# Row LSTM with group norm on one core: part of the second half's first row moved ahead of the last image's statistics, and late work in another order

## The chip, the cores and the metric

One core of a Trainium2 chip runs the whole program. The metric is the device time of one execution in microseconds; lower is better. Four executions of the kernel before give a median of 2064.85 us (2064.63 to 2064.95).

## The reference, cut to what matters

The input x has 8 images of 96 channels, 128 rows and 128 columns, all float32. It is group-normalised (32 groups of 3 channels), convolved along each row with a masked 3-tap filter, and then a convolutional LSTM runs down the 128 rows, one row after another:

```
its = conv(gn(x), W_is * mask) + b_is          # 1 x 3 along a row, 384 gate channels
def step((h, c), row):                          # 128 steps, each needs the one before
    gates = conv(h, W_ss) + b_ss + row          # 3 taps along the row
    f, i, o = sigmoid(...); g = tanh(...)
    c = f * c + i * g
    h = o * tanh(c)
out = x + h of every row
```

The scale and shift of the group norm need the sums of a whole image. So no row of an image can be normalised before all of that image has been read once.

## The kernel before, in words

The 8 images are split into two halves of four (`s` = 0 and 1). A half step `n` is one row of one half: `n = 2 * row + s`. The two halves take turns, so that the gates of one are evaluated while the products of the other run. The 384 gate channels are three tiles A, B, C of 128 rows, each in a PSUM bank of 512 columns: two transforms of 4 images x 64 column pairs, 256 columns each ("half 0" and "half 1" of the bank).

For every tile of a half step there are seven products, each a matmul over 256 columns (4 images x 64), and each of them two instructions on TensorE (PE). `P`, `Q` and `E` (`p_`, `q_`, `t_`) multiply the own part of the normalised input, kept in `xs`; they use 64 of the 128 rows of the array, and two of them on different rows run side by side. `1`, `2`, `0`, `3` (`m1_`, `m2_`, `m0_`, `m3_`) multiply operands made from the previous row's h and the shared part of the input, kept in `hx`: `vs` (sum, `total`, L496), `vf` (difference, `difference`, L500) and `vd` (`shifted`, L504). All products go through `HalfStep.mm` and stand on L390. Then `cp` copies half 0 with its bias, `lo` (L439) and `hi` (L443) combine the halves, and `0`, `3` are added after `lo` and `hi`. `ta` and `si` are the gate functions on ScalarE (ACT), `gt` the product of gates, `th` and `ou` give the new h.

The order on PE, ACT, VectorE (DVE) and GpSimd (POOL) is the order of the program; nothing reorders it. A list such as `"1A 2A PA"` is run by `do(n, names)`; `+` means the next half step and `*` the one after that. So `P*A`, called with n = 1, is the product P for tile A of half step 3, the second row of the second half.

The program has two parts. First all 8 images are read once for their sums (a loop over 8 images and 24 chunks of 512 columns each; DVE's `bn_stats`, L760, and ACT share the chunks). Beside it `events[at(image, chunk)]` places other work: while images 4 to 7 are read, half steps 0 and 2 are begun with the first half's images. Image 7 is the last one; before it is done, the scale of images 4 to 6 is made (`begin_scale`, `squares`, `next_row`), and three of four images of the second half get their first row (`next_operands`, `own_row(..., 0, BH - 1)`).

TensorE is also given products that nobody reads: `spin(count, rhs)` (L174), 256 columns each, into a bank that half step 1 later overwrites; `keep_warm(count)` puts one narrow product in front that waits for the newest record of the statistics.

When image 7's sums are aggregated (`st`, L674), its scale is made. The chain is short instructions on two engines: `final.deviations()` (PE, `dm<-st`, L251), `variance_and_square` (DVE, L272), `variances` and `means` (PE, `pv`, `dm`, L251), `scale` (eight instructions of DVE, L279 to L286), then the last image's shared input (DVE, L782) and its part of `vs` and `vf`. After that the products of half step 1 start. Meanwhile ACT widens the last image's first row (`xw`, L295) and rows 1 to 3 of all four images (`rows`, L295, tile `piece`), and POOL makes the last image's `xs` and `vd`, normalises the shared part of rows 1 to 3 for four images (`shared_rows(nc.gpsimd, 1, 1, R)`, L297, tile `hx`), and combines rows 1, 2 and 3 to `xs` (`own_row`, L315 and L316).

From half step 3 on, a fixed order (`PERIOD`, `PRODUCTS`) repeats to the end.

Of the kernel before, what the change touches and what calls it, by code (L numbers as in the profile page):

```python
# [21 lines left out]
def kernel(  # L22
# [32 lines left out]
    nc = tc.nc  # L55
    B, C, H, W = x.shape
    P = 128
    NH = 2
    BH = B // NH
    R = 4  # L60
    NB = H // R
    J = W // 2
# [23 lines left out]
    wt = [tap[1], wm[:, 0, :], wm[:, 1, :], tap[2]]  # L86
# [44 lines left out]
    xw = [const.tile([P, R, W + 1], F32, tag=f"xw{i}", name=f"xw{i}") for i in range(2)]  # L131
# [29 lines left out]
    E = mybir.EngineType  # L161
# [7 lines left out]


    def spin(count, rhs):
        unread = half_step(1).ps[0]
        for i in range(count):
            nc.tensor.matmul(  # L174
                unread[:, 0 : rhs.shape[1]],
                wt[0][:, 0:P],
                rhs,
                start=True,
                stop=True,
                skip_group_check=True,  # L180
            )

    def first_rows(s, homes=(0, 1, 2)):

        hi = 1 if s else R
        t = xt[s, 0].rearrange("c b r w -> c b (r w)")[:, :, 0 : hi * W]
        own, shared = (x0[:, 0], x0[C:P, 1]) if s else (xr[s], t[C:P])
        for i in homes:
            if i == 2:
                nc.scalar.activation(shared, t[C2:C], AF.Identity)  # L190
            else:
                nc.scalar.activation(own[i * C2 : (i + 1) * C2], t[0:C2], AF.Identity)
# [33 lines left out]
    class Scale:  # L226


        def __init__(self, s, lo, hi, banks=None):
            n, self.name = hi - lo, f"{s}_{lo}"  # L230
            self.st, self.rstd, self.nmr = (
                st[s][:, lo:hi], rstd[s][:, :, lo:hi], nmr[s][:, :, lo:hi]
            )


            self.first, at = banks is None, 0 if banks is None else 3 * BH
            self.banks = banks or [bank(f"{name}{self.name}") for name in ("dm", "pv")]
            self.dm, self.pv = (
                own[:, at : at + i * n].rearrange("p (i b) -> p i b", i=i)
                for own, i in zip(self.banks, (3, 2))  # L240
            )
            self.pm = self.dm[:, 1:3, :]
            self.q, self.t, self.minus = (
                const.tile([P, *shape], F32, name=f"{name}{self.name}")
                for name, shape in (("q", [n]), ("t", [2, n]), ("minus", [2, n]))
            )
            for i in range(2):
                self.mm(self.pv[:, i, :], i, eps[:, 0:n], start=self.first and i == 0)

        def mm(self, o, i, rhs, start=False, stop=False):  # L250
            nc.tensor.matmul(o, gm[:, i, :], rhs, start=start, stop=stop, skip_group_check=True)  # L251
# [47 lines left out]
    def widen(engine, xw, i, n, s, k, j, lo, step=1):  # L299


        norm(
            engine,
            strided(xw[:, i, :], 0, [(step * (W + 1), n), (J + 1, 2), (1, J)]),
            (x0[:, 0, j] if s == 1 and k == lo == 0 else xr[s][:, j, lo * W : (lo + n) * W])
            .rearrange("p (r j t) -> p r t j", r=n, t=2),
            0,
            1,
            s * BH + j,
        )  # L310

    def combine(xw, n, total, differences):

        e, o = xw[:, 0:n, 0:J], xw[:, 0:n, J + 1 :]
        nc.gpsimd.tensor_add(total, e, o)  # L315
        nc.gpsimd.tensor_sub(  # L316
            differences,
            strided(xw[:, 0, :], 0, [(W + 1, n), (J, 2), (1, J)]),
            strided(xw[:, 0, :], J + 1, [(W + 1, n), (0, 2), (1, J)]),
        )  # L320
# [7 lines left out]
    def own_row(xw, s, r, lo=0, hi=BH):  # L328

        to = xs[s][0]  # L330
        combine(
            xw[:, lo:hi],
            hi - lo,
            to[:, r, 0, lo:hi],
            to[:, r, 1:3, lo:hi].rearrange("p t b j -> p b t j"),
        )

    def normalise_shared(engine, s, k, j, lo, hi):

        norm(  # L340
            engine,
            strided(
                hx[s][k % 2][C:P, lo, 0, j, :],
                0,
                [(2 * BH * JP, hi - lo), (BH * JP + 1, 2), (1, J)],
            ),
            (x0[C:P, 1, j : j + 1] if s == 1 and k == lo == 0 else xt[s, k][C:P, j, lo:hi, :])
            .rearrange("p r (j t) -> p r t j", t=2),
            C,
            0,  # L350
            s * BH + j,
        )

    HB = BH * J
    NT = NB * R
    last = NT * NH - 1
    order = {"A": 0, "B": 1, "C": 2}
# [4 lines left out]
    class HalfStep:  # L362


        def __init__(self, n):
            self.n, (self.row, self.s) = n, divmod(n, NH)
            self.ps, self.m1, self.moving, self.done, self.gates = {}, {}, {}, set(), None
            self.started = set()
            self.hx = hx[self.s][self.row // R % 2][:, self.row % R]
            self.xs = xs[self.s][self.row // R % 2][:, self.row % R]  # L370
            self.c = cs[self.s].rearrange("p t b j -> p (t b j)")
# [14 lines left out]
        def mm(self, a, half, weights, rhs, rows=slice(0, P)):  # L386
            self.take_bank(a)
            new = a not in self.started
            self.started.add(a)
            nc.tensor.matmul(  # L390
                self.ps[a][:, bass.ts(half, HB)],
                weights[rows, bass.ts(a, P)],
                rhs[rows],
                start=new,
                stop=False,
                skip_group_check=True,
            )
# [170 lines left out]
    def finish(n):  # L568
# [22 lines left out]
    PARTS = {  # L591
        "P": "p_", "Q": "q_", "E": "t_", "1": "m1_", "2": "m2_", "0": "m0_", "3": "m3_",
        "cp": "copy", "lo": "even", "hi": "odd", "ta": "tanh", "si": "sigmoid",
        "fg": "forget", "gt": "gated", "ce": "cell", "th": "cell_tanh", "ou": "output",
        "S": "total", "F": "difference", "D": "shifted", "re": "residual",
    }
    steps = {}

    def half_step(n):
        if n not in steps:  # L600
            steps[n] = HalfStep(n)
        return steps[n]

    def do(n, names):

        for name in names.split():
            at = n
            for mark, offset in (("'", -1), ("+", 1), ("*", 2)):
                if mark in name:
                    at, name = n + offset, name.replace(mark, "")  # L610
            tile_ = name[-1] if name[-1] in order else ""
            part = name[: len(name) - len(tile_)]

            if part in ("S", "F", "D"):
                at += NH
            if not 0 <= at <= last:
                continue
            step = half_step(at)
            if name not in step.done:
                step.done.add(name)  # L620
                getattr(step, PARTS[part])(*([order[tile_]] if tile_ else []))
# [15 lines left out]
    def shared_rows(engine, s, lo, hi, images=range(BH)):  # L637
        for j in images:
            normalise_shared(engine, s, 0, j, lo, hi)
# [30 lines left out]
    def at(image, n):  # L670
        return image * NS + n
# [4 lines left out]
    def next_products():  # L676
# [5 lines left out]
            half_step(1).take_bank(a)  # L682
        do(2, "PA PB QA QB PC QC 1A 2A 1B 2B 1C 2C")

    def begin_scale():
        late[0].deviations()
        late[0].variances(late[0].st[:, :, 1])
# [6 lines left out]
    def keep_warm(count):  # L694
        spin(1, bst[:, done - 1, :])
        spin(count, wt[0][:, 0:256])
# [16 lines left out]
        ),  # L713
        at(6, 8): lambda: (do(0, "gt th ou"), operands(2), do(0, "re")),
        at(6, 9): next_products,
        at(6, 17): lambda: keep_warm(6),
        at(6, 22): lambda: (first_rows(1), do(2, "cpA cpB cpC")),
        at(7, 5): begin_scale,
        at(7, 7): squares,
        at(7, 8): lambda: (next_row(), spin(14, wt[0][:, 0:256])),  # L720
        at(7, 12): next_operands,
        at(7, 20): lambda: (own_row(xw[1], 1, 0, 0, BH - 1), keep_warm(2)),
        at(7, 22): lambda: keep_warm(2),
    }
    for b in range(B - 1):
# [43 lines left out]
    rows = ring[2][:, 0 : (R - 1) * BH * (W + 1)].rearrange("p (r q) -> p r q", q=W + 1)  # L769
# [4 lines left out]
    final.variance_and_square()  # L774
    final.variances(final.q)
    final.means()
    spin(4, wt[0][:, 0:256])
    nc.scalar.activation(final.minus, final.pm, AF.Identity, scale=-1.0)
    final.scale()
    nc.gpsimd.tensor_mul(final.nmr, final.minus, final.rstd)  # L780
# [9 lines left out]
    step = half_step(1)  # L790
# [6 lines left out]

    for j in range(BH):
        widen(nc.scalar, rows, j, R - 1, 1, 0, j, 1, step=BH)
    shared_rows(nc.gpsimd, 1, 1, R)  # L800
    for r in range(1, R):
        own_row(rows[:, (r - 1) * BH : r * BH], 1, r)
    load_rows(0, 1)
    for s in range(NH):
# [2 lines left out]

    do(1, "1A 2A 1B 2B 1C 2C PA PB QA QB E+A PC E+C QC P*A E+B cpA cpB cpC loA loB loC")  # L810
    do(1, "EA P*B Q*A EB EC Q*B hiA hiB hiC 0A 3A 0B 3B 0C 3C taA taB siB taC siC")
    finish(0)
    do(1, "gt th 0+A 3+A 0+B 3+B 0+C 3+C ou F S D re")
    finish(1)
# [9 lines left out]
    step, halves = half_step(last), [(0, BH // 2), (BH // 2, BH)]  # L824
# [62 lines left out]
```

## Time and profile before

| | |
|---|---|
| median of four executions | 2064.85 us |
| the profiled execution | 2065.23 us, span 2063.5 us |
| PE busy | 1961.2 us, 95% of the span |
| DVE, POOL, ACT busy | 1678.0, 1450.3, 1364.2 us |
| PE's last unbroken stretch | from 153.59 us on, 1899.64 us |
| mean granted TensorE clock | 0.996 |

The span is the time from the first to the last instruction of the profiled execution; 1.7 us of its time lie outside. Line numbers are those of the kernel before. A matmul of the program is two instructions in the profile.

### The profile page before, as it was taken

To read this page: it belongs to the slowest core of one execution; us is meant where nothing else is said; L and a number is where in the kernel's file an instruction comes from. 1 tells how busy PE (TensorE), PEld (TensorE's weight loads), DVE (VectorE), ACT (ScalarE), POOL (GpSimd) and SP (SyncE) were. 2 spreads that over 40 slices of the span, in tenths; PEclk is the share of its full clock that TensorE was granted. 3 is DMA by queue.
4 is the path that set the end of the run, shared out by engine and by line. 5 is a ranking of instruction groups with operands and counts; after the bars stand their busy time and mean duration, and the time that the engine had idled before them with its cause. 6 is when DMAs were issued, how large, how long until landed. Compare 5 with 4: busy or idle time off the path is not lost.

```text
span 2063.5 us, 31403 instructions
## 1 busy us (share of the span) xinstructions
PE 1961.2 (95%) x10866; PEld 1597.4 (77%) x10866; DVE 1678.0 (81%) x3489; ACT 1364.2 (66%) x2403; POOL 1450.3 (70%) x1652
## 2 busy tenths in 40 slices
PE   0389999999999999999999999999999999999998
PEld 0268888888888888888888888888888888888886
DVE  5768888888888888888888888888888888888887
ACT  4776666666666666666666666666666666666666
POOL 3348777777777777777777777777777777777762
PEclk9989999999999999999999999999999999999999
DMA  9994333444333344433334443333444333344411
GB/s 382 424 308 89 94 87 87 109 113 113 94 76 87 87 109 113 113 93 77 87 88 107 113 113 93 77 88 87 107 113 113 96 74 88 88 107 113 113 31 31
DMA packets 103325, 236.26 MB, mean 114 GB/s; under 512 B 5952, under 2 KB 8896, under 8 KB 97280
## 3 DMA queue, kind: packets, MB, share of 16 engines
q1 hardware_dynamic: 103168, 234.25, 41.2%
q8 instruction: 88, 1.44, 0.3%
q14 instruction: 69, 0.57, 0.1%
HBM read 183.90 MB, written 50.33 MB: 114 GB/s over the span
## 4 chain that ended last, share of the span: by engine, by line
PE 94%; DMA 3%; DVE 1%; POOL 1%; ACT 0%; issue 0%; SPq 0%; DVEq 0%; POOLq 0%
PE ps L390 93%; DMA xs<-in_x_dram 3%; DVE bst L760 1%; PE ps L174 1%; POOL xs L315 0%; POOL xs L316 0%; POOL xw L297 0%; SPq L748 0%; POOL hx L297 0%; PE pv L251 0%; ACT xs L217 0%; ACT xs L216 0%; ACT g L446 0%; PE dm L251 0%; ACT ps L453 0%
## 5 line engine op out<-in xcount | busy, mean ns | idle before, releaser
L390 PE MATMUL ps<-vd,wl 128*128 128x256 f32 x3072 | 814.3, 388 | 0.0
L446 ACT ACTIVATE g<-ps 32x512 f32<-32x512 f32 x768 | 454.3, 592 | 449.7 <-PE ps L390 441.6
L390 PEld LDWEIGHTS ps<-vd,wl 128*128 128x128 f32 x3072 | 562.4, 190 | 151.2 <-issue 85.1
L504 POOL TENSOR_TENSOR vd<-hx 128x512 f32<-128x512 f32 x257 | 266.8, 1038 | 460.4 <-DVE vs L496 459.4
L390 PE MATMUL ps<-xs,wx 64*128 64x256 f32 x3072 | 459.4, 395 | 11.0 <-POOL xs L315 11.0
L390 PE MATMUL ps<-vs,wm 128*128 128x256 f32 x1536 | 458.9, 381 | 4.5 <-POOL vs L496 4.4
L390 PE MATMUL ps<-vf,wm 128*128 128x256 f32 x1536 | 458.6, 380 | 0.0
L453 ACT ACTIVATE ps<-ps 96x512 f32<-96x512 f32 x766 | 417.7, 572 | 16.2
L390 PEld LDWEIGHTS ps<-xs,wx 64*128 64x128 f32 x3072 | 323.7, 187 | 119.7 <-issue 83.6
L458 DVE TENSOR_TENSOR ps<-ps,c 96x512 f32<-96x512 f32 x254 | 176.7, 696 | 257.5 <-ACT ps L453 257.4
L443 DVE TENSOR_TENSOR ps<-m,ps 128x256 f32<-128x256 f32 x768 | 329.2, 429 | 26.9 <-PE ps L390 0.7
L522 POOL TENSOR_TENSOR x<-x,hx 96x512 f32<-96x512 f32 x255 | 331.0, 1298 | 5.7 <-DVE hx L483 5.7
L439 DVE TENSOR_TENSOR ps<-m,ps 128x256 f32<-128x256 f32 x768 | 325.1, 424 | 8.9
L390 PEld LDWEIGHTS ps<-vs,wm 128*128 128x128 f32 x1536 | 292.6, 191 | 46.1 <-POOL vs L496 5.4
L390 PEld LDWEIGHTS ps<-vf,wm 128*128 128x128 f32 x1536 | 292.7, 191 | 40.8 <-DVE vf L500 0.4
L436 ACT ACTIVATE m<-ps,wl 128x256 f32<-128x256 f32 x514 | 243.9, 475 | 74.7 <-PE ps L390 61.3
L316 POOL TENSOR_TENSOR xs<-xw 128x512 f32<-128x512 f32 (+1 forms) x254 | 270.7, 1066 | 0.0
L390 PE MATMUL ps<-xs,wt 64*128 64x256 f32 x1530 | 264.5, 376 | 0.1
L476 ACT ACTIVATE th<-c 96x512 f32<-96x512 f32 (+1 forms) x257 | 161.8, 630 | 105.7 <-DVE c L471 104.3
L297 POOL TENSOR_SCALAR hx<-x,rstd,nmr 32x512 f32<-32x512 f32 (+1 forms) x252 | 204.8, 813 | 25.9
L297 POOL TENSOR_SCALAR xw<-xr,rstd,nmr 128x512 f32<-128x512 f32 x252 | 203.7, 808 | 7.7 <-DVE nmr L289 6.7
L390 PEld LDWEIGHTS ps<-xs,wt 64*128 64x128 f32 x1530 | 195.0, 187 | 18.0 <-issue 0.7
(91 smaller groups left out, 1302.2 us busy)
## 6 DMA issues: line engine op xcount, KB each, us to landing
xr<-in_x_dram SPq DMA_DIRECT2D x124, 512.0 KB, 6.4
x<-in_x_dram SPq DMA_DIRECT2D x63, 768.0 KB, 5.9
out_dram<-x SPq DMA_DIRECT2D x62, 768.0 KB, 4.9
xs<-in_x_dram SPq DMA_DIRECT2D x30, 1024.0 KB, 12.4
piece<-in_x_dram SPq DMA_DIRECT2D x16, 1024.0 KB, 12.3
x<-in_x_dram SPq DMA_DIRECT2D x62, 256.0 KB, 3.1
xs<-in_x_dram SPq DMA_DIRECT2D x4, 512.0 KB, 8.5
out_dram<-x SPq DMA_DIRECT2D x2, 576.0 KB, 3.7
```

Of the source, the lines that this page charges most:

```text
L297: engine.tensor_scalar(dst, src, scale, shift, ALU.mult, ALU.add)
L316: nc.gpsimd.tensor_sub(differences, strided(xw[:, 0, :], 0, [(W + 1, n), (J, 2), (1, J)]), strided(xw[:, 0, :], J + 1, [(W + 1, n), (0, 2) ...
L390: nc.tensor.matmul(self.ps[a][:, bass.ts(half, HB)], weights[rows, bass.ts(a, P)], rhs[rows], start=new, stop=False, skip_group_check=True,)
L436: nc.scalar.activation(self.m1[a], m1, AF.Identity, bias=column)
L439: nc.vector.tensor_add(self.ps[a][:, 0:HB], self.m1[a], self.ps[a][:, HB:])
L443: nc.vector.tensor_sub(hi, self.m1[a], hi)
L446: nc.scalar.activation(self.g[a * 32 : (a + 1) * 32], self.ps[a][C:P], AF.Tanh)
L453: nc.scalar.activation(gate, gate, AF.Sigmoid)
L458: nc.vector.tensor_mul(f, f, self.c)
L476: nc.scalar.activation(self.part(self.th, lo, hi), self.part(self.c, lo, hi), AF.Tanh)
L504: diff = nc.gpsimd.tensor_sub(self.operand("vd", 2)[:, :, lo:hi], strided(h, 1, [(BH * JP - 1, 2), (JP, hi - lo), (1, J)]), strided(h, 0, ...
L522: (nc.gpsimd if 2 * row + s < last else nc.vector).tensor_add(xo, xo, self.h)
```

## The change

Seven edits, all around the end of the statistics:

1. `spin` writes to the bank of tile C of half step 1, no longer of tile A.
2. `keep_warm` in image 6 runs 14 unread products, no longer 6.
3. New: `early(names)` runs products of half step 1 on images 0 to 2 alone (192 columns), and leaves the fourth image (64 columns) for the place where the product stood before. At `at(7, 20)` it runs `1A 2A 1B 2B` in place of `keep_warm(2)`.
4. Behind the last image's `means`, `early("PA PB QA QB")` and two unread products stand in place of four.
5. POOL's order: the shared rows of images 0 and 1, then `own_row` of row 1, then the shared rows of images 2 and 3, then rows 2 and 3.
6. The list of half step 1 is split, so that tiles A and B return to 256 columns behind `QB`.
7. Half step 1 runs `hi`, `0`, `3` and the gate functions in the order B, A, C, no longer A, B, C.

```diff
     def spin(count, rhs):
-        unread = half_step(1).ps[0]
+        unread = half_step(1).ps[2]
...
-            self.started = set()
+            self.started, self.images = set(), {}
...
+            lo, hi = self.images.get(a, (0, BH))
+            cols = slice(lo * J, hi * J)
             nc.tensor.matmul(
-                self.ps[a][:, bass.ts(half, HB)],
+                self.ps[a][:, bass.ts(half, HB)][:, cols],
                 weights[rows, bass.ts(a, P)],
-                rhs[rows],
+                rhs[rows, cols],
...
+    def early(names):
+
+        step = half_step(1)
+        for name in names.split():
+            step.images[order[name[1]]] = (0, BH - 1)
+            getattr(step, PARTS[name[0]])(order[name[1]])
+            step.images[order[name[1]]] = (BH - 1, BH)
...
-        at(6, 17): lambda: keep_warm(6),
+        at(6, 17): lambda: keep_warm(14),
...
-        at(7, 20): lambda: (own_row(xw[1], 1, 0, 0, BH - 1), keep_warm(2)),
+        at(7, 20): lambda: (own_row(xw[1], 1, 0, 0, BH - 1), early("1A 2A 1B 2B")),
...
     final.means()
-    spin(4, wt[0][:, 0:256])
+    early("PA PB QA QB")
+    spin(2, wt[0][:, 0:256])
...
-    shared_rows(nc.gpsimd, 1, 1, R)
-    for r in range(1, R):
+    shared_rows(nc.gpsimd, 1, 1, R, range(0, 2))
+    own_row(rows[:, 0:BH], 1, 1)
+    shared_rows(nc.gpsimd, 1, 1, R, range(2, BH))
+    for r in range(2, R):
         own_row(rows[:, (r - 1) * BH : r * BH], 1, r)
...
-    do(1, "1A 2A 1B 2B 1C 2C PA PB QA QB E+A PC E+C QC P*A E+B cpA cpB cpC loA loB loC")
-    do(1, "EA P*B Q*A EB EC Q*B hiA hiB hiC 0A 3A 0B 3B 0C 3C taA taB siB taC siC")
+    do(1, "1A 2A 1B 2B 1C 2C PA PB QA QB")
+    half_step(1).images.clear()
+    do(1, "E+A PC E+C QC P*A E+B cpA cpB cpC loA loB loC")
+    do(1, "EA P*B Q*A EB EC Q*B hiB hiA hiC 0B 3B 0A 3A 0C 3C taB siB taA taC siC")
```

## The prediction, made before the changed kernel ran

> **What bounds the kernel now.** I read the chain of waits first, in order of time, because it shows where the place of the change lies on the path.
>
> ```profile
> span 2063.5 us, 31403 instructions
> 125.04 11.34 PE ps L174 x40
> ...
> 144.97 8.59 PE ps L390 x46
> 153.56 0.03 issue
> 153.59 1899.64 PE ps L390 x10600
> ```
>
> Columns are start, length, what. From 153.59 us the chain is PE alone. In the single records behind it, neighbouring half steps take 7.74 and 7.31 us in turn to the end, and no two matmuls start more than 0.33 us apart. So this part is set by PE, and the change leaves its instructions and their order as they are: it moves as a block, by as much as its start moves. What counts is when the first product of half step 3 starts, now 153.59. Ahead of it, 11.34 us of the chain are products that nobody reads (L174). So I looked at PE and DVE there, each in order of time (start, length; in brackets the idle time before and what ended it):
>
> ```profile
> 124.90 9.30 PE L174 MATMUL ps<-wl 128*128 128x256 f32 x28
> 134.04 0.28 PE L174 MATMUL ps<-bst,wl 128*128 128x6 f32 x2
> 136.21 0.28 PE L251 MATMUL dm<-st,wl 128*128 128x1 f32 x2
> 137.33 0.58 PE L251 MATMUL dm<-st,wl 128*128 128x1 f32 x4
> 139.90 0.67 PE L390 MATMUL ps<-vs,wm 128*128 128x256 f32 x2 [0.15 <-DVE vf L500]
> 144.97 0.48 PE L390 MATMUL ps<-xs,wx 64*128 64x256 f32 x1 [0.31 <-POOL xs L315]
> ```
>
> and on DVE:
>
> ```profile
> 133.31 0.63 DVE L674 BATCH_NORM_AGGREGATE st<-bst 128x2 f32<-128x105 f32 x1
> 136.53 0.28 DVE L272 TENSOR_SCALAR q<-dm,st 128x1 f32<-128x1 f32 x1 [2.59 <-PE dm L251]
> ```
>
> The last image's statistics are there at 133.94 (133.31 + 0.63), but `dm`, which needs them, starts at 136.21: it stands behind the unread products in PE's queue, and DVE idles 2.59 us. Why the queue is late is seen in the granted clock, cut in slices of 1 us (length; busy time of PE, PEld, DVE, ACT, POOL; clock; DMA):
>
> ```profile
> 117.00:118.00 1.00, 0.70 (x4) 0.27 (x2) 1.00 (x2) 1.00 (x3) 0.00 (x0) 1.00 0.99 410
> 121.00:122.00 1.00, 0.08 (x1) 0.12 (x1) 1.00 (x3) 0.76 (x2) 0.00 (x0) 0.50 1.00 426
> 130.00:131.00 1.00, 1.00 (x3) 0.74 (x3) 1.00 (x3) 0.97 (x3) 1.00 (x4) 0.50 0.14 57
> 131.00:132.00 1.00, 1.00 (x6) 0.89 (x5) 1.00 (x3) 0.91 (x2) 0.89 (x4) 1.00 0.34 77
> ```
>
> PE ends image 6's unread products at 117.70 and idles to 121.92. The clock falls to half at 120.8 and stays there to 131.0, so most of the 28 spin instructions start 0.427 us apart, not 0.216. The second thing on the path is the 144.97 row: `P*A` waits for POOL, whose own order holds it up:
>
> ```profile
> 139.82 3.05 ACT L295 ACTIVATE piece<-xr,nmr,rstd 128x384 f32<-128x384 f32 x4
> ```
>
> and on POOL:
>
> ```profile
> 141.13 3.06 POOL L297 TENSOR_SCALAR hx<-x,rstd,nmr 32x384 f32<-32x384 f32 x4
> 144.27 0.64 POOL L315 TENSOR_TENSOR xs<-piece 128x256 f32<-128x256 f32 x1
> ```
>
> The rows that L315 needs leave ACT at 142.87; POOL makes four `hx` first.
>
> **Edit 2, eight more unread products in image 6.** 16 instructions x 0.216 = 3.45 us: PE is busy to 117.70 + 3.45 = 121.15 instead of 117.70, and idles 0.8 us before `dm` of images 4 to 6 (121.92), which they do not delay. The four changes of the clock here (110.5, 113.9, 120.8, 131.0) are 3.41 us or multiples of it apart. The steps of 3.41 us with PE idle for 3 us or more lowered it; the one from 103.7 with 1.1 us idle did not. So I take the clock as kept. The short matmuls then take 0.112 us each (137.33 row: 0.45 for four starts) and not 0.213 as at 122 to 125. The spin starts at about 123.6 and ends at about 129.7. If the clock does fall at 124.2, one full step raises it (110.5 to 113.9 did), and the spin ends at 131.3. [...]
>
> **Edit 3, `1A 2A 1B 2B` on three images, ahead.** Eight instructions of 192 columns, 0.75 x 0.216 = 0.162 each, 1.3 us. `vs` and `vf` of three images leave POOL at 130.07 and 130.65, so these end at 131.9 (132.6 with a clock that fell). Behind them the remaining `keep_warm` waits for DVE's statistics (131.95) and takes 0.22 + 4 x 0.216 = 1.1 us: PE is free at 133.1 to 133.7. Statistics to `dm` took 0.15 us in the earlier case (121.77 to 121.92). So `dm` starts at 133.94 + 0.15 = **134.08, 2.13 us earlier**. DVE's statistics do not move: they wait at 129.43 for the DMA. The chain from `dm` to `1A` keeps its links and its 3.69 us, so `1A` starts at 137.77. DMAs that this uncovers: the row data for ACT was issued by 130.8 and landed within 5.7 us, the `x` piece for `hx` at 131.5 and 6.0 us later: 136.5 and 137.5, needed at 137.7 and 139.0. The 512 KB of the next rows land at 144.7, needed at 147. SP's queue is in the same order; only its last load starts with ACT's earlier end.
>
> **Edit 4, `PA PB QA QB` ahead and two spins fewer.** Between `means` and `1A`: 0.65 + 0.86 instead of 1.73 us, hidden behind DVE's `scale`; `xs` of three images is there at 133.6. If that cover were gone it would cost nothing more than the spins it replaces.
>
> **What the early products save on PE.** The 64 columns left of `1` and `2` cost between 0.054 (a quarter of 0.216) and 0.112 per instruction; I take 0.112, since the nearest row is the short matmuls with a new weight load each. [...] By my row `1A 2A 1B 2B` fall from 1.73 to 0.90 us. `PA PB QA QB` fall from 0.97 to 0.45 (loads side by side) or 0.90 (one by one). From `1A`: 0.90 + 0.86 (1C, 2C) + 0.45 to 0.90 + 0.86 (E+A, PC, E+C, QC) + 0.2 for changes of shape = 3.3 to 3.7. PE is ready for `P*A` at 141.1 to 141.5.
>
> **Edit 5, POOL's order.** `own_row` of row 1 now waits for two `hx` (ended at 142.61 before) and ACT's rows (142.87), so it can start at 142.93 instead of 144.27, **1.34 us earlier** relative to the chain: 142.93 - 2.13 = 140.80, ends 141.44, `P*A` at 141.50. That is later than PE is ready, or just equal: what the early products save on PE is mostly waited away. The two `hx` put behind L316 are needed by half step 3 at 150, when POOL is long done; POOL stood idle 2.29 us before its next `vd`.
>
> **Edit 7, B first.** `hiB` waits for `EB`, which stands behind `Q*A` and so behind L316: before, `hiB` started 1.80 after `P*A` and took 0.43; so `0B` starts 2.27 after `P*A`, where `0A` started 2.085 after it: 0.19 lost. The gates gain: `taA`, `taB`, `siB`, `taC` with a wait of 0.27 become `taB siB taA taC` without. But before, PE was ready at 153.49, only 0.09 ahead of `vf`; so 0.09 of that gain is seen, and then PE is the bound: **+0.10**. Edits 1 and 6 move no time by themselves.
>
> **Sum.** -2.13 - 1.34 + 0.10 = -3.37 us against the profiled execution: 2065.23 - 3.37 = 2061.86. That execution lies 0.38 above the median, so I predict 2061.48, rounded **2061.5**, -0.16%. A measurement of this kernel can tell about 0.2%, 4.1 us, from no change; the forecast is just inside. Its own range is 2060.9 to 2062.1, from the bounds of the narrow products, the 0.15 us start of `dm`, and `hiB`.
>
> **Rivals.** *The clock is not kept* (0.11). If the clock stays at half from 124.2 to 131.0, as it did although PE had been busy from 124.9, the spin ends at 133.0, the early products at 134.3, `keep_warm` at 135.4: `dm` gains 0.81, not 2.13. Time 2061.5 + 1.32 = 2062.8. For it: one full-looking step before did not raise the clock. Against: the idle time that lowered it is filled. *All ends are favourable* (0.20). The loads run side by side, `P*A` comes with PE's 141.1 rather than POOL's 141.5, `hiB` is not late, and the shorter gate chain is all used: 0.4 + 0.2 + 0.2 more, 2060.7 or a little less, over the bound of 0.2%. Against: L315 needs all four widened images. *The moved work waits elsewhere* (0.06). If a transfer for ACT or POOL lands 2 us later than before, the gain of `dm` goes there: 2063.5. *Slower* (0.06): PE now idles 0.6 us before `1A` and does narrow work before that; if this lowers the clock at 137.8 for as long as it stayed low before, 10.2 us, half of that is lost, 5.1 - 3.4 = +1.7: 2066.6. It decides from 6.8 us of half clock on. Against: spins still stand there. The forecast has 0.57.
>
> **Numbers.** The range 2060.2 to 2063.5 takes in the forecast, the first rival, the transfer that comes late and half of the favourable case; 0.16 is left out. Faster by over 0.2% needs the favourable case: 0.22 with a little for what I do not see. Slower by over 0.2%: 0.04. The rest, 0.74, is within 0.2%.
>
> **What would show it.** Right: clock 1.0 from 114 on; `dm<-st` 128x1 at about 134.1; `1A` (128x64) at 137.8; L315 at 140.8 straight behind ACT; `P*A` at 141.5 behind a short wait for POOL; the unbroken PE stretch from about 150.2 and as long as before, 1899.6. Wrong: a half clock after 124, a wait for a DMA at `piece` or `hx`, or another length of the last stretch.

## The result and the profile after

| | before | after |
|---|---|---|
| median | 2064.50 us (52 runs, 2062.09 to 2069.27) | 2062.19 us (34 runs, 2061.19 to 2066.47) |
| profiled execution | 2065.23 us, span 2063.5 | 2064.12 us, span 2062.3 |

The ratio is 0.9990, with a 95% interval of 0.9985 to 0.9994: 2.3 us less, inside the 0.2% that were named as no clear change, and clear of zero. The predicted 2061.5 us is 0.7 us below the median. The profiled execution of after is one of its slower ones, 1.9 us above its median; in it the clock falls, and that turned out to be the key to the case.

The page and the chain of waits of after, in order of time (start, length, what):

```profile
span 2062.3 us, 31445 instructions
145.97 1906.16 PE ps L393 x10630
```

PE again carries all that follows; L393 is the old L390. From half step 3's first product to the end it takes 1909.59 us (1909.57 before). What changed lies ahead of it. PE in order of time:

```profile
114.84 6.29 PE L174 MATMUL ps<-wl 128*128 128x256 f32 x28
122.59 0.36 PE L251 MATMUL dm<-st,wl 128*128 128x3 f32 x2 [1.47 <-DVE st L677]
124.69 9.27 PE L174 MATMUL ps<-wl 128*128 128x256 f32 x28
133.80 0.49 PE L393 MATMUL ps<-vs,wm 128*128 128x192 f32 x2
136.18 0.28 PE L251 MATMUL dm<-st,wl 128*128 128x1 f32 x2
139.79 0.43 PE L393 MATMUL ps<-vs,wm 128*128 128x64 f32 x2
143.69 0.48 PE L393 MATMUL ps<-xs,wx 64*128 64x256 f32 x1 [0.36 <-POOL xs L315]
152.46 0.70 PE L393 MATMUL ps<-vf,wm 128*128 128x256 f32 x2
```

The eight more unread products fill PE to 121.1, as they should. But the 28 spin instructions behind 124.69 take 9.27 us, as long as before, and `dm` starts at 136.18: not earlier at all, although the statistics are there at 133.60 (132.97 + 0.63), on DVE:

```profile
132.97 0.63 DVE L677 BATCH_NORM_AGGREGATE st<-bst 128x2 f32<-128x105 f32 x1
```

The clock, in slices of 1 us (columns as in the prediction: length; busy time of PE, PEld, DVE, ACT, POOL; clock; DMA):

```profile
121.00:122.00 1.00, 0.13 (x1) 0.00 (x0) 1.00 (x3) 0.38 (x3) 0.00 (x0) 1.00 1.05 442
124.00:125.00 1.00, 1.00 (x6) 1.00 (x6) 0.82 (x5) 1.00 (x3) 0.27 (x1) 0.50 1.03 434
130.00:131.00 1.00, 1.00 (x5) 0.82 (x4) 1.00 (x3) 1.00 (x1) 0.96 (x3) 0.63 0.16 66
```

It no longer falls at 120.8; it falls one step later, at 123.9, and rises at 130.7. On ACT and POOL:

```profile
139.80 3.05 ACT L295 ACTIVATE piece<-xr,nmr,rstd 128x384 f32<-128x384 f32 x4
142.99 0.64 POOL L315 TENSOR_TENSOR xs<-piece 128x256 f32<-128x256 f32 x1 [0.41 <-ACT piece L295]
```

L315 of row 1 stands straight behind ACT's rows now, and `P*A` (143.69) 1.28 us earlier than before. So in this execution nearly all of the gain, 1.02 of 1.11 us, is behind `1A`, half step 1's first product behind the scale (139.79): 13.68 us from `1A` to half step 3 (152.46) before, 12.66 now.

### The profile page after: what moved, and what is told of

It reads as the page before. It is cut to its first block, busy times and chain, and to the rows that moved or that the text cites. A ratio compares the mean times of both kernels' runs of the same rounds, so it can differ in the third digit from the quotient of the medians.

```text
span 2062.3 us, 31445 instructions
## 1 busy us (share of the span) xinstructions
PE 1962.6 (95%) x10888; PEld 1598.8 (78%) x10888; DVE 1676.2 (81%) x3489; ACT 1362.2 (66%) x2403; POOL 1446.9 (70%) x1652
## 4 chain that ended last, share of the span: by engine, by line
PE 93%; DMA 4%; ACT 2%; DVE 1%; issue 0%; SPq 0%; POOL 0%; DVEq 0%; POOLq 0%
PE ps L393 93%; DMA piece<-in_x_dram 3%; DMA xs<-in_x_dram 1%; PE ps L174 1%; ACT piece L216 1%; ACT piece L217 0%; DVE bst L771 0%; ACT hx L295 0%; ACT piece L295 0%; ACT xs L216 0%; ACT xs L217 0%; ACT g L449 0%; SPq L759 0%; PE pv L251 0%; PE dm L251 0%
## 5 line engine op out<-in xcount | busy, mean ns | idle before, releaser
L393 PE MATMUL ps<-vd,wl 128*128 128x256 f32 x3072 | 814.3, 388 | 0.1
L393 PEld LDWEIGHTS ps<-vd,wl 128*128 128x128 f32 x3072 | 562.4, 190 | 151.3 <-issue 84.7
L393 PE MATMUL ps<-xs,wx 64*128 64x256 f32 x3080 | 459.9, 394 | 11.0 <-POOL xs L315 11.0
L393 PE MATMUL ps<-vs,wm 128*128 128x256 f32 x1540 | 459.5, 380 | 4.3 <-POOL vs L499 4.3
L393 PE MATMUL ps<-vf,wm 128*128 128x256 f32 x1540 | 458.8, 380 | 0.0
L393 PEld LDWEIGHTS ps<-xs,wx 64*128 64x128 f32 x3080 | 324.0, 187 | 119.7 <-issue 83.9
L393 PEld LDWEIGHTS ps<-vs,wm 128*128 128x128 f32 x1540 | 293.1, 191 | 45.7 <-POOL vs L499 5.4
L393 PEld LDWEIGHTS ps<-vf,wm 128*128 128x128 f32 x1540 | 293.3, 191 | 40.6 <-DVE vf L503 0.4
L316 POOL TENSOR_TENSOR xs<-xw 128x512 f32<-128x512 f32 (+1 forms) x254 | 270.3, 1064 | 0.0
L393 PE MATMUL ps<-xs,wt 64*128 64x256 f32 x1530 | 264.6, 377 | 0.3 <-DVE ps L446 0.3
L393 PEld LDWEIGHTS ps<-xs,wt 64*128 64x128 f32 x1530 | 195.0, 187 | 18.2 <-DVE ps L446 0.7
```

The source lines that it names most:

```text
L316: nc.gpsimd.tensor_sub(differences, strided(xw[:, 0, :], 0, [(W + 1, n), (J, 2), (1, J)]), strided(xw[:, 0, :], J + 1, [(W + 1, n), (0, 2) ...
L393: nc.tensor.matmul(self.ps[a][:, bass.ts(half, HB)][:, cols], weights[rows, bass.ts(a, P)], rhs[rows, cols], start=new, stop=False, skip_g ...
```

## The experiments

Theory Q: two hold-ups, one behind the other. PE's queue of unread products, whose length the clock sets (28 instructions took 9.27 us in after, where the clock fell), delays `dm`; POOL's order delays `P*A`. Rival R: all of the gain is POOL's order. Later a second part was added: the clock's steps of 3.41 us lie differently against the program from one execution to another (the same kernel lost the clock at 120.8 us in before and at 122.8 in before_again), so the first hold-up differs too.

The times of single executions scatter by some 2 us, more than most of these effects. So each experiment is read by four distances from the single records of its profile, beside its times. "Aggregate" is the end of L674's last instruction (L677 after), when the last image's statistics are there; `dm` is the start of PE's first instruction that uses them. "End" is the end of POOL's last clearing of semaphores, 0.3 us ahead of the end of the span in every profile.

| kernel | aggregate ends | to `dm` | `1A` to half step 3 | half step 3 to the end | half clock, 118 to 140 | median (before, measured beside it) | ratio, 95% |
|---|---|---|---|---|---|---|---|
| before | 133.94 | 2.27 | 13.68 | 1909.57 | 120.8-131.0 | 2064.50 | |
| before_again | 134.48 | 1.72 | 13.71 | 1909.58 | 122.8-129.6 | 2065.56 (2064.74) | 0.9993-1.0013 |
| before_spin8 | 134.21 | 0.05 | 13.70 | 1909.58 | 123.5-130.3 | 2062.85 (2064.74) | 0.9982-1.0000 |
| pool_alone | 132.94 | 1.82 | 12.96 | 1909.84 | 121.4-128.2 | 2064.69 (2064.81) | 0.9993-1.0010 |
| after | 133.60 | 2.58 | 12.66 | 1909.59 | 123.9-130.7 | 2062.19 (2064.50) | 0.9985-0.9994 |
| after_again | 136.21 | 0.05 | 12.68 | 1909.64 | none | 2062.60 (2064.71) | 0.9979-0.9997 |
| pool_undone | 135.64 | 2.22 | 13.87 | 1909.57 | 124.5-131.4 | 2063.45 (2064.81) | 0.9985-1.0003 |
| warm6 | 133.45 | 2.89 | 12.69 | 1909.97 | 120.6-130.8 | 2063.98 (2064.71) | 0.9986-1.0004 |
| warm19 | 134.02 | 0.05 | 12.70 | 1909.60 | none | 2062.70 (2064.81) | 0.9982-1.0000 |
| spin8 | 134.84 | 0.05 | 12.70 | 1909.58 | none | 2062.28 (2064.81) | 0.9978-0.9996 |
| no_early | 133.61 | 0.06 | 13.06 | 1909.57 | none | 2062.53 (2064.71) | 0.9978-0.9998 |
| order_abc | 134.21 | 0.76 | 12.67 | 1909.56 | 124.9-128.3 | 2062.37 (2064.71) | 0.9977-0.9997 |
| row_first | 133.82 | 0.05 | 11.84 | 1910.37 | none | 2062.19 (2064.74) | 0.9979-0.9997 |
| row3_late | 133.72 | 0.29 | 11.82 | 1909.98 | none | 2061.78 (2064.33) | 0.9979-0.9997 |

From `dm` to `1A` it is 3.60 to 3.80 us in all of them.

**POOL's order, done alone and undone.** pool_alone is the kernel before with edit 5; pool_undone is after without it.

```diff
-    shared_rows(nc.gpsimd, 1, 1, R)
-    for r in range(1, R):
+    shared_rows(nc.gpsimd, 1, 1, R, range(0, 2))
+    own_row(rows[:, 0:BH], 1, 1)
+    shared_rows(nc.gpsimd, 1, 1, R, range(2, BH))
+    for r in range(2, R):
         own_row(rows[:, (r - 1) * BH : r * BH], 1, r)
```

> The kernel before with POOL's new order alone (the shared rows of images 0 and 1, own_row of row 1, then the rest). Theory Q (the end of PE's queue of unread products sets the start of the last image's scale, and POOL's order is a second, separate hold-up): L315 of row 1 starts right behind ACT's widened rows, 1.3 us earlier than before, and P*A with it; dm 128x1 stays at about 136.2. Half step 3 starts 1.2 to 1.3 us earlier: about -1.25 us, ratio 0.9994. Rival R (all of the change's gain is POOL's order): -2.3 us, as much as the whole change. If neither order of POOL matters, 0.

> The changed kernel with POOL's old order. Theory Q: P*A waits again behind four hx, 1.3 us later than in the changed kernel when dm starts at the same time; so +1.3 us against the changed kernel, about -1.0 us against before in the median, and in an execution whose clock falls as in the profile shown, 0 against before. Rival R: no gain left at all, 0 against before in the median too.

Alone it takes 0.72 us off the way from `1A` to half step 3, not 1.25: PE has its full products there and does not pause between `1A` and half step 3, so it is the bound by then. 0.27 us are lost again behind half step 3 (1909.84); where, I did not follow up. The times show no difference (0.9993 to 1.0010). Rival R is out: it asked for 2.3 us less, 0.9989, and the order alone is not the gain. Without it, the rest of the change gains nothing on this way (13.87 against 13.68); PE, early by then, waits for POOL (pool_undone, PE in order of time):

```profile
146.62 0.48 PE L393 MATMUL ps<-xs,wx 64*128 64x256 f32 x1 [1.62 <-POOL xs L315]
```

So edit 5 and the rest, the early products above all, need each other on this way: edit 5 alone -0.72 us, all the others without it +0.19, together -1.02.

**A shorter queue, and a kept clock.** Two edits of after: spin8 turns the 14 unread products behind the scale of images 4 to 6 into 8, warm19 the 14 of image 6 into 19.

```diff
-        at(7, 8): lambda: (next_row(), spin(14, wt[0][:, 0:256])),
+        at(7, 8): lambda: (next_row(), spin(8, wt[0][:, 0:256])),
```
```diff
-        at(6, 17): lambda: keep_warm(14),
+        at(6, 17): lambda: keep_warm(19),
```

> The changed kernel with 8 unread products instead of 14 behind the scale of images 4 to 6. Theory Q: PE's queue is empty before the statistics are, whether the clock falls or not: with a fallen clock 7 products to 130.7, one more, then the early products to 132.5 and the narrow product for DVE to 133.6. dm 128x1 starts 0.15 us behind the aggregate of image 7, about 133.8 instead of 136.2; all that follows moves up by 2.2 to 2.4 us; L315 of row 1 at 140.7. Against the changed kernel -2.3 us where its clock falls, about -1.2 us in the median of its executions (some of which I take to keep the clock). Rival D (a transfer takes its place): the row data for ACT or the x piece for POOL lands later than 137.5, so piece or hx waits for a DMA, and less than 1 us is gained. Rival H (the clock): with fewer unread products the clock falls behind 134 and the real products run at half speed, +1.7 us or more.

> The changed kernel with 19 unread products in image 6 instead of 14, so that PE is busy to about 123.3 and the clock's step from 120.5 to 124.0 is 80% full. Theory Q with the clock as its cause: the clock stays at 1.0 from 114 on, the 14 products behind the scale run at 0.216 us an instruction from about 125 and end by 131.1, dm 128x1 at about 133.8. The same gain as with 8 products in the queue, -2.3 us where the changed kernel's clock falls. Rival: the clock falls at 124 all the same, since the short matmuls at 123 to 125 do not count as work; then dm starts at 136.2 or later, and the time is that of the changed kernel or 0.7 us more.

Both put `dm` 0.05 us behind the aggregate. In warm19 the clock does not fall between 118 and 140, and PE's order of time shows what that is worth:

```profile
118.74 4.70 PE L174 MATMUL ps<-wl 128*128 128x256 f32 x21
124.91 6.29 PE L174 MATMUL ps<-wl 128*128 128x256 f32 x28
134.08 0.38 PE L251 MATMUL dm<-st,wl 128*128 128x1 f32 x2
```

28 instructions in 6.29 us instead of 9.27. In spin8's profile the clock did not fall either, so it does not show the short queue under a fallen clock; before_spin8 does. No DMA took the place of the wait (rival D), and the clock did not fall behind 134 (rival H). From the aggregate to half step 3 both take 16.45 us, 2.4 less than after's first profile. The times are 2.1 and 2.5 us below before, with intervals that do not part them from after. For spin8 that is a miss: it was expected some 1.2 us below after in the median, and 2062.28 stands beside 2062.19 and, in the next experiment, 2062.60; warm19 has 2062.70. The distances show what the queue costs where the clock falls; the times do not show how often it falls.

**The change once more, and with image 6 as before.** warm6 is after with `keep_warm(6)`.

> The changed kernel once more, unchanged, for a second profile and times beside the next three. Theory Q+phase: the clock's steps of 3.41 us lie anywhere against the program (the six profiles so far have them 0.66 to 1.96 us into a step at the start of the span), so whether a step between 119 and 127 is idle enough to lower the clock differs from execution to execution. Then dm starts 0.06 us behind the aggregate of image 7 where the clock is kept, and 2.2 to 2.6 us behind it where it falls at about 124. From 1A to half step 3 it takes 12.67 to 12.70 us either way (13.68 before). Median -2.3 us against before. Rival: the clock always falls at about 124, and the queue always holds dm up by 2.2 us or more; then the -2.3 us in the median must come from somewhere else.

> The changed kernel with 6 unread products in image 6, as before. Theory Q+phase: PE is idle from about 117.7 to 122, which holds nearly a whole step of 3.41 us wherever the steps lie; the clock falls near 121 and PE's queue holds dm up by 1.5 to 2.5 us in nearly every execution. From 1A on all is as in the changed kernel (12.7). Median 1 to 1.3 us above the changed kernel, that is about -1.1 us against before. Rival: the eight products do nothing, and the median is the changed kernel's.

after_again is the same kernel as after, and its clock is kept from 119 us on (PE in order of time):

```profile
127.14 6.29 PE L174 MATMUL ps<-wl 128*128 128x256 f32 x28
136.27 0.38 PE L251 MATMUL dm<-st,wl 128*128 128x1 f32 x2
```

`dm` follows the aggregate by 0.05 us, not 2.58. That this execution is no faster as a whole is the input: its statistics were ready 2.6 us later. warm6 has the half clock from 120.6 to 130.8 and the longest queue of all; its median is 1.4 us above after_again's, measured beside it. So the extra products are worth about that in the median, though they did nothing in after's first profile; the size is rough, since the intervals of the two ratios overlap.

**Without early products; with the old late order.** In no_early `keep_warm(2)` and `spin(4)` return and the products of `1A` to `QB` are whole again; order_abc returns to `hiA hiB hiC 0A 3A 0B 3B 0C 3C taA taB siB taC siC`.

```diff
-        at(7, 20): lambda: (own_row(xw[1], 1, 0, 0, BH - 1), early("1A 2A 1B 2B")),
+        at(7, 20): lambda: (own_row(xw[1], 1, 0, 0, BH - 1), keep_warm(2)),
...
-    early("PA PB QA QB")
-    spin(2, wt[0][:, 0:256])
+    spin(4, wt[0][:, 0:256])
```

> The changed kernel without early products: keep_warm(2) and four unread products as before, 1A to QB on 256 columns in their old place; the rest of the change stays. Theory Q: what the early products take off PE behind 1A is 1.2 to 1.3 us, of which all but 0.3 us is waited away for L315 of row 1 (the changed kernel's PE waits 0.43 us for it, and 0.19 us for hiB). From 1A to half step 3: about 13.0 us instead of 12.7 (it is 12.96 with POOL's order alone). Rival E (the early products carry the gain): 13.7 or more.

> The changed kernel with half step 1's late order A, B, C instead of B, A, C. Theory Q: 0A starts 2.09 us behind P*A (0B: 2.28 us), and the gate functions finish 0.27 us later relative to it; the two cancel to within 0.1 us: from 1A to half step 3 12.6 to 12.8 us. Rival: the order B, A, C is worth its 0.27 us, and it takes 12.95 us or more.

no_early loses 0.4 us from `1A` to half step 3 (13.06): that is all that remains of the 1.28 us that PE saves there (its first product behind `QB` starts 2.45 us behind `1A` in after, 3.73 before). Its median, 2062.53, is that of after_again (2062.60). order_abc: 0.20 us earlier at the first `0`, 0.20 later behind it, 12.67 in sum; the order B, A, C is worth nothing here.

**The kernel before with one number changed, and once more.** before_spin8 is before with `spin(8, ...)` at `at(7, 8)`.

> The kernel before with 8 unread products instead of 14 behind the scale of images 4 to 6, and nothing else. Theory Q: the clock falls near 121 as before, but PE's queue is empty in time: dm 0.05 to 0.3 us behind the aggregate instead of 1.8 to 2.3; 1A to half step 3 stays at 13.7. From the aggregate to half step 3 17.4 to 17.7 us instead of 19.65; median about -1.9 us, nearly the whole gain of the change with one number. Rival (the clock): the queue is shorter, but the clock stays at half behind 131, and less than 1 us is gained.

> The kernel before once more, for a second profile. Theory Q+phase: the clock falls near 121 again (PE is idle from 117.7 to 122, longer than one step), dm stands 1.5 to 2.5 us behind the aggregate, 13.7 us from 1A to half step 3; the end of the input's reading moves by 1 us or more against the first profile. Rival: the clock is kept in this execution, dm at 0.05 us; then the queue is no steady cost of the kernel before.

PE in order of time, before_spin8:

```profile
125.57 6.06 PE L174 MATMUL ps<-wl 128*128 128x256 f32 x16
134.26 0.38 PE L251 MATMUL dm<-st,wl 128*128 128x1 f32 x2 [0.47 <-DVE st L674]
```

The clock falls (123.5 to 130.3), 16 instructions take 6.06 us, and PE is still ready 0.47 us before the statistics. That is the queue shown by itself: from the aggregate to half step 3 it takes 17.56 us, 19.65 before: 2.1 us of the profile before were a wait for unread products. The median is 1.9 us lower. In all 11 executions the mean granted clock is 0.995 or 0.996, as before: the clock is no better, only the queue is shorter. One number gives most of what the seven edits give (2.3 us). before_again shows the queue a second time, 1.72 us.

**A step further.** row_first is warm19 with row 1 widened and combined ahead of all else; row3_late also moves row 3 behind half step 3's sum.

```diff
     for j in range(BH):
-        widen(nc.scalar, rows, j, R - 1, 1, 0, j, 1, step=BH)
...
+        widen(nc.scalar, rows, j, 1, 1, 0, j, 1)
+    own_row(rows[:, 0:BH], 1, 1)
+    shared_rows(nc.gpsimd, 1, 1, R)
...
+    do(1, "E+A PC E+C QC P*A E+B cpA cpB cpC")
+    for j in range(BH):
+        widen(nc.scalar, rows, BH + j, R - 2, 1, 0, j, 2, step=BH)
```

> Warm19 (19 unread products in image 6) with row 1 widened first: ACT widens row 1 of the four images, then copies for tiles B and C, then widens rows 2 and 3; POOL combines row 1 ahead of all four hx, rows 2 and 3 behind them. Theory Q: 5.9 us from 1A on, when ACT's 12 rows used to be ready, no longer matter: L315 of row 1 starts at 1A + 1.7 us instead of + 3.2, P*A comes with PE at 1A + 3.4 instead of + 3.9, Q*A no longer waits for L316. 1A to half step 3 in 11.9 to 12.1 us instead of 12.7, dm 0.05 us behind the aggregate: 15.7 to 15.9 us from the aggregate to half step 3. Against before about -3 us in the median. Rival W (ACT and POOL are late elsewhere): rows 2 and 3 push ACT's gate functions or POOL's next vd back, and 1A to half step 3 stays at 12.7 or grows.

> Row_first with POOL's own_row of row 3 moved behind vd and the residual sum of half step 3. In row_first 0.82 us was gained from 1A to half step 3 and 0.79 us lost again right behind it, where DVE's vs ran beside POOL's L316 and took 1.29 us instead of 0.42. Theory S (the two engines slow each other there): POOL is idle from about 3.0 us before vs, vs takes 0.42 us again, the wait of PE for it is gone, and from half step 3 to the end it takes 1909.6 us; the aggregate to the end 1925.2 us instead of 1926.0 (warm19, row_first). Median about -0.8 us against row_first, -3.4 us against before, ratio 0.9984. Rival P (POOL's work as a whole is the bound): the late row moves POOL's next vd back, PE waits for that, and 1910.0 us or more remain.

row_first takes 11.84 us from `1A` to half step 3, a little less than expected, and gives 0.77 us back right behind it. DVE, POOL and PE of row_first in order of time:

```profile
149.29 1.29 DVE L499 TENSOR_TENSOR vs<-hx 128x256 f32<-128x256 f32 x1
```
```profile
149.04 1.25 POOL L316 TENSOR_TENSOR xs<-xw 128x512 f32<-128x512 f32 x1
```
```profile
150.63 0.70 PE L393 MATMUL ps<-vs,wm 128*128 128x256 f32 x2 [0.51 <-DVE vs L499]
```

`vs` runs beside POOL's L316 and ends only behind it; in row3_late POOL is idle there, 1.22 us up to its `vd` (DVE in order of time):

```profile
149.14 0.42 DVE L499 TENSOR_TENSOR vs<-hx 128x256 f32<-128x256 f32 x1
155.59 0.84 DVE L503 TENSOR_TENSOR vf<-hx 128x256 f32<-128x256 f32 x1
```

0.42 instead of 1.29; but half a period later `vf` meets the next L316 (155.09 to 156.15), and half of the loss stays: 1909.98. From the aggregate to the end row3_late takes 1925.7 us, warm19 1926.05, after 1928.4 and 1926.1, before 1929.2. Its median is the lowest of all, 2061.78, but its ratio to before, 0.9988 (0.9979 to 0.9997), does not part it from after. Expected were 0.8 us less than row_first and 3.4 less than before; the medians give 0.4 and 2.55.

## Why the prediction was right, and where its steps were not

The median, 2062.19, lies in the range, and "within 0.2%" was right. In part that is luck. The sum forecast 3.35 us less than before; measured are 2.31, and 3.35 lies outside the interval (1.2 to 3.1). The time came nearer than the difference because the 52 executions of before have a median 0.35 us below the four from which the sum started, and the range had room for the first rival. Step by step:

- *"So I take the clock as kept."* This step failed in the profile of after, and with it the term -2.13 us: `dm` moved from 2.27 to 2.58 us behind the aggregate. The first rival was the right one there, but dearer than its 1.32 us: it let the spin start at 123.6, and it started at 124.69; 0.7 us of that are the statistics of image 6, which came later in this execution, the rest short matmuls that took longer than forecast. What the step had wrong: it took the clock's steps to lie as in the profile before, and PE's short matmuls to be enough to keep the clock. In after one step runs from 120.5 to 123.9; unread products fill 0.63 us of it and short matmuls 1.30, and the clock fell behind it. The term counts as an average. Of the five profiles with PE's work of after up to `spin(14)` (after, after_again, pool_undone, no_early, order_abc) three had a half clock; `dm` stood 2.58, 0.05, 2.22, 0.06 and 0.76 us behind the aggregate, 1.13 in the mean. The four with 6 products in image 6 and 14 behind the scale (before, before_again, pool_alone, warm6) had it all: 1.72 to 2.89, 2.18 in the mean. So the term is about -1.05, not -2.13, if five profiles stand for all executions.
- *POOL's order, -1.34 us.* The mechanism was right; it measured -1.17: from `1A` to L315 4.37 us before, 3.20 after. POOL started 0.15 us behind ACT's last row, and `1A` came 0.08 us nearer to `dm`, ahead of ACT.
- *B first, +0.10 us.* `0B` came 2.28 us behind `P*A` (forecast 2.27) and half step 3 6.49 us behind that: +0.15.
- *The early products are mostly waited away.* Right: PE stood idle 0.36 us for `P*A`, and no_early lost 0.4 us. The products of 64 columns took 0.112 us an instruction, as taken; the eight of `PA PB QA QB` ran side by side, 0.49 us until the next (forecast 0.45 to 0.90).
- *The last stretch moves as a block.* Right to 0.1 us in after and after_again.

-1.05 - 1.17 + 0.15 = -2.07, beside the measured -2.31 (-3.1 to -1.2 by the interval). What share of all executions keeps the clock was not counted; five profiles are few, and the mean granted clock of each execution does not tell: 32 of after's 34 and all 11 of after_again have 0.997, the profile whose clock fell at 123.9 and the one that kept it among them. So the first term's average, and with it the match of the sum, stays open.

## What to carry to other kernels

Work that only keeps an engine warm stands in its queue like any other: size it for the slow clock (28 unread instructions took 9.27 us in after and 6.29 in after_again, whose clock was kept), and put it so that the queue is empty when the critical input arrives (in warm19 and spin8 `dm` follows the aggregate by 0.05 us, in after by 2.58). One profile is one draw; where the clock and the input's reading differ between executions (here the statistics were ready between 132.94 and 136.21 us), compare distances between events of one execution, not times of day. And before a wait is removed, ask who is next: here POOL's order alone was worth 0.7 us on the way to half step 3, the other edits less than nothing there, both 1.0 us together, and 0.77 us of a third gain, in row_first, were handed back to two engines: DVE's `vs` took 1.29 us beside POOL's L316 and 0.42 without it.

## What the runs showed of the hardware that was not expected

In the traces the clock's changes lie 3.41 us or a multiple of it apart: 110.5, 113.9, 120.8 and 131.0 us in before, 110.3, 113.7, 123.9 and 130.7 in after. The stretches at half clock in the table are 3.4, 6.8 or 10.2 us long, to 0.1 us. Against the program's start they lie differently from execution to execution: before and before_again, the same kernel, lost the clock 2.0 us apart.

In before, half clock followed the steps from 107.1 and 117.4, in which PE was busy 0.16 and 0.30 of 3.40 us; behind the one from 103.7, with 2.28, the clock stayed full. In after half clock followed the step from 120.5, with 1.93 us busy, 0.63 of it unread products and 1.30 short matmuls of 3 columns. In order_abc the unread products ended at 122.08, short matmuls stood from 123.05 to 124.77, and the clock fell at 124.9. In after PE was busy throughout the step from 123.9 to 127.3, and the clock stayed at half for one more: so 6.8 us at half clock (123.9 to 130.7) stand behind a single step of 3.41 us. What share of a step decides, these steps do not show.

The end of the statistics, which follow the reading of the input, differs by 3.3 us between the profiles (aggregate from 132.94 to 136.21), more than the whole change.

DVE's `vs` took 1.29 us beside POOL's L316 in row_first and 0.42 alone in row3_late; that L316 took 1.25 us, the next one (154.50) 1.07. In row_first `vs` began 0.25 us behind L316 and ended 0.29 us behind it. In row3_late `vf` took 0.84 us beside its L316 and ended 0.28 us behind it; half a period earlier, with POOL idle, it took 0.43. The cause of the longer times is not shown.
